# A graph layer's gathers: more columns fetched row by row on two queues, and edge features loaded for two groups at a time

## The chip, the cores and the metric

One core of a Trainium2 chip runs the whole kernel. A core has five engines with instruction streams of their own: TensorE (PE in the profile; its weight loads are shown as PEld), VectorE (DVE), ScalarE (ACT), GpSimd (POOL) and SyncE (SP, which does no arithmetic here and issues transfers). ScalarE, SyncE and GpSimd issue DMA transfers between HBM and the on-chip memory. The metric is the device time of the whole kernel in microseconds, the median of several runs.

## What is computed

A graph of 12,500 nodes with 64 features each and 200,000 edges, sorted by destination. Each edge makes a message from its two nodes' features and its own; messages are added up by destination, and the nodes are updated and normalised.

```python
def ssp(x): return jax.nn.softplus(x) - jnp.log(2.0)
nodes = node_state[edges].reshape(num_edges, -1)          # [x[src], x[dst]], 128 wide
gates = ssp(edge_state @ We1 + be1) @ We2 + be2
soft_cutoff = 1.0 - jax.nn.sigmoid(5.0 * (edges_distance - (CUTOFF - 1.5)))
h = ssp(nodes @ Wn1 + bn1) @ Wn2 + bn2
messages = h * gates * soft_cutoff
message_sum = jnp.zeros_like(node_state).at[edges[:, 1]].add(messages)
new_state = node_state + (ssp(message_sum @ Ws1 + bs1) @ Ws2 + bs2)
return layernorm(node_state + new_state)
```

## The kernel before

**Groups and columns.** The edges are cut into 391 groups of 512 (`NG`, `GE`). A group has two halves `h` of 256 edges and is laid out as `K = 4` columns of 128 edges. For a column, 128 rows of x are needed, one for each edge's source, 64 floats each. The main loop runs one step `i` for each group, with several groups in different stages in one step.

**Preparation** (the first 80 us or so) builds a table of x times the lower half of Wn1 in HBM (`table`), from which a window of 42 destination rows is loaded for each half of a group (`wns`, L235): since edges are sorted by destination, the destinations of a half lie within 42 nodes. During the preparation the gathers of the first 14 groups (`AHEAD`) are issued too.

**Fetching source rows.** Most columns are gathered by GpSimd: one indirect DMA for each column (`gather`, L202), reading 128 indices from `src_i`. In the main loop step `i` issues the gathers of group `i + 14`; the tile `xg` has 18 buffers. Some columns, listed by `slots_by_rows` (L101), are not gathered: column 3 of groups 36, 68, ... 388 is fetched by single rows on SyncE's queue and column 2 of the same groups on ScalarE's. `fetch(i, engine)` (L206) loads four row numbers into registers (L215) and issues four DMAs of one row (256 bytes) each (L219). SyncE's four stand behind the loads of the step; ScalarE's are split, two between the exp and the log of a step and two between the log and the copy behind it. A column takes 32 steps and is used from step g - 3 on; group 36's last rows are issued in step 31. ScalarE's rows are issued only in steps below 380 (`ends`).

**Loading.** `load(g)` (L225), called in step g - 5, issues on SyncE the edge features `eT` of one group (L228, 128 KB) and the two windows `wns` (L235), whose row numbers come from registers loaded for two groups at a time (L230). The loads wait until the scatter of group g - 11 is done.

**The order of a step**, written out by hand, for i < 380:

- SyncE: `load(i + 5)`, then four rows. GpSimd: the gathers of group i + 14.
- TensorE: `layer2_edge(i - 1)`, whose first matmul is L293; `layer1_edge(i + 1)` and `layer1_node(i + 1)` (L260, L262, L268); the scatter of group i - 3 (L320, a matmul with a one-hot matrix); `transposes(i + 3)` (L251); `layer2_node(i - 1)` (L303).
- L293 takes the waits of the step in one place (`needs`): the copy and the loads of group i + 1, and the gathers and one-hot of group i + 3.
- ScalarE: exp of group i + 1 (L279), two rows, log (L282), two rows, the copy of the transposed group i + 3 (`xcopy`, L256).
- VectorE: cutoff and message (L312, L316), the window's addition (L337), softplus (L287), the one-hot of group i + 5 (L241, and L244 for the columns fetched by rows).

Node blocks of 512 nodes (25 in all) are worked off between these, when the sums of their nodes are complete: a load and a store on SyncE's queue (L362, L416), some matmuls, and some work on ScalarE and VectorE. In the last ten steps (`CATCH_UP`) the lags shrink and the order changes, so that all stages end together; the last groups and the last node block follow the loop.

**Completion semaphores** of DMAs come from a pool: transfers issued by SyncE and ScalarE share some of them, and a new issue on a semaphore waits until the earlier transfer on it has landed.

Of the kernel before, what the change touches and what calls it, by code (L numbers as in the profile page):

```python
# [32 lines left out]

# [3 lines left out]

# [5 lines left out]
F32 = mybir.dt.float32  # L43
BF16 = mybir.dt.bfloat16
I32 = mybir.dt.int32
# [11 lines left out]
P = 128  # L57
D = 64
HE = 256
# [5 lines left out]
K = 4  # L65
# [7 lines left out]


BLOCK_STEPS = ((2, 3, 4, 4, 6, 7, 8, 9, 10, 14), (2, 3, 3, 4, 5, 6, 7, 8, 9, 10), (1, 2, 1, 2, 3))
ROWS = 4
CUTOFF = 5.0
EPS = 1e-5
LN2 = 0.6931471805599453
# [18 lines left out]
    return steps  # L98


def slots_by_rows(NG):  # L101

    return [(g, k) for k in (K - 1, K - 2) for g in range(P // ROWS + 4, NG - 2, P // ROWS)]


@with_exitstack
def gnn_resnorm_kernel(ctx: ExitStack, tc: tile.TileContext, a: dict, out: bass.AP, E: int):
    nc = tc.nc
    x = a["x"]
    N = x.shape[0]  # L110
    NG = a["eT"].shape[1]
# [8 lines left out]
    const = ctx.enter_context(tc.tile_pool(name="const", bufs=1))  # L120
    dram = ctx.enter_context(tc.tile_pool(name="dram", bufs=1, space=DRAM))
    loads = ctx.enter_context(tc.tile_pool(name="loads", bufs=LOADS + 2))
# [26 lines left out]
    packed, at = {}, 0  # L149
# [18 lines left out]
    xgs, xrs, eTs = {}, {}, {}  # L168
    made = {}

    def note(key, ins):
        made.setdefault(key, []).append(ins)
        return ins

    def behind(ins, *keys):

        for key in keys:
            for other in made.get(key, []):
                tc.add_manual_dep(ins.ins, other.ins.name,
                                  mybir.DependencyInfo(mybir.DependencyClass.Sync, mybir.DependencyReason.DATA),  # L180
                                  reason="one place of a step takes its waits")

    by_rows = slots_by_rows(NG)
    rows_i = const.tile([len(by_rows), P], I32, name="rows_i")
    half_of = {nc.sync: 0, nc.scalar: len(by_rows) // 2}

    def padding(g, k):
        return g * GE + k % 2 * HE + k // 2 * P >= E
# [14 lines left out]
                out=xg[:, k, :D], out_offset=None, in_=x,  # L203
                in_offset=bass.IndirectOffsetOnAxis(ap=src_i[:, g, k : k + 1], axis=0)))

    def fetch(i, engine, first=0, count=ROWS):  # L206

        n, r = divmod(i * ROWS + first, P)
        if i < 0 or n >= len(by_rows) // 2:
            return  # L210
        n += half_of[engine]
        if r == 0:
            xrs[by_rows[n]] = loads.tile([P, P], F32, name=f"xr{by_rows[n][1]}", bufs=2)
        if first == 0:
            _, row_at[engine] = nc.values_load_multi_w_load_instructions(  # L215
                rows_i[n : n + 1, r : r + ROWS], engines=[engine.engine], min_val=0, max_val=N - 1,
                skip_runtime_bounds_check_because="src holds rows of x")
        for j in range(count):
            note(("gather", by_rows[n][0]), engine.dma_start(xrs[by_rows[n]][r + j : r + j + 1, :D],  # L219
                                                             x[bass.ds(row_at[engine][first + j], 1), :]))  # L220

    row_at = {}
    bases = {}

    def load(g):  # L225
        eTs[g] = loads.tile([P, HE], F32, name="eT")
        old = ("scatter", g - LOADS - 2 - 4)
        behind(note(("load", g), nc.sync.dma_start(eTs[g], a["eT"][:, g, :])), old)  # L228
        if g % 2 == 0:
            _, at = nc.values_load_multi_w_load_instructions(  # L230
                base_i[0:1, 2 * g : 2 * g + 4], engines=[SP], min_val=0, max_val=N - 1,
                skip_runtime_bounds_check_because="they were clamped to these bounds")
            bases[g], bases[g + 1] = at[:2], at[2:]
        for h in range(2):
            behind(note(("load", g), nc.sync.dma_start(wns[D:DW, g % REST, h, :], table[bass.ds(bases[g][h], W), :])),  # L235
                   old)
# [17 lines left out]
    def xcopy(g):  # L254
        xT = work.tile([DW, K, P], F32, name="xT", bufs=3)
        note(("xcopy", g), nc.scalar.copy(xT, xTs[g]))  # L256
        xTs[g] = xT.rearrange("f (t h) e -> f h t e", h=2)
# [169 lines left out]
    with tc.manual_schedule():  # L427
# [4 lines left out]
        with tc.tile_pool(name="prep", bufs=1) as prep:  # L432
# [10 lines left out]

            for i in range(3):
                load_x(i)
            nc.sync.dma_start(rows_i, a["rows"])
            dist = cut.rearrange("p g k -> p (g k)")
            nc.sync.dma_start(dist, a["dist_l"])
            dst_i = rel.bitcast(I32)
# [50 lines left out]
            for i, w in enumerate((we2[:D, 0, :], wn2)):  # L500
                n = w.shape[0]
# [16 lines left out]
            rows = prep.tile([PIECES, 4, D], BF16, name="rows")  # L518
# [6 lines left out]
            for i in range(PARTS):  # L525
# [19 lines left out]
                if i == 2:  # L545
# [5 lines left out]
                    for t in range(2):  # L551
                        r = rel[:, :, 2 * t : 2 * t + 2]
# [3 lines left out]
        with tc.tile_pool(name="finish", bufs=1) as finish:  # L556
# [14 lines left out]
            parts, begun, complete, rest = {}, None, 0, []  # L571
# [9 lines left out]
            for i in range(-3, last - 1):  # L581
                now = parts.pop(i, [])
                early = [part for part in now if part.tensor]
                at(load, i + LOADS)
                fetch(i, nc.sync)
                if i >= 0:
                    at(gather, i + AHEAD, i < BEHIND)
                if i < ends:
                    needs = [("xcopy", i + 1), ("load", i + 1)]
                    needs += [(name, g) for g in ahead[i] for name in ("gather", "onehot")]  # L590
                    for g in second[i]:
                        layer2_edge(g, *needs)
                    if i >= -1:
                        zs[i + 1] = z_tile()
                        layer1_edge(i + 1)
                        for part in early:
                            part.tensor(tx_tile())
                    if i >= -1:
                        layer1_node(i + 1)
                    for n, g in enumerate(third[i]):  # L600
                        scatter(g, zs[i + 1][:, 1, HE + 2 * W * n : HE + 2 * W * (n + 1)])
                    at(exps, i + 1)
                    fetch(i, nc.scalar, 0, ROWS // 2)
                    at(logs, i + 1)
                    fetch(i, nc.scalar, ROWS // 2, ROWS // 2)
                    for g in ahead[i]:
                        transposes(g)
                        xcopy(g)
                    for g in second[i]:
                        layer2_node(g)  # L610
                    for g in second[i]:
                        hcut(g)
                        message(g)
                    for g in third[i]:
                        window(g)
                    for part in early:
                        part.others()
                    at(softplus, i + 1)
                else:
                    for g in ahead[i]:  # L620
                        transposes(g)
                        xcopy(g)
                    zs[i + 1] = z_tile()
                    layer1_edge(i + 1)
                    for part in early:
                        part.tensor(zs[i + 1][:, 1, HE:])
                    layer1_node(i + 1)
                    exps(i + 1)
                    logs(i + 1)
                    for g in second[i]:  # L630
                        layer2(g)
                        hcut(g)
                        message(g)
                    softplus(i + 1)
                    for g in third[i]:
                        scatter(g, tx_tile()[:, : 2 * W])
                        window(g)
                    for part in early:
                        part.others()
                for g in ahead[i]:  # L640
                    at(onehot, g + 2)
                for part in now:
                    if not part.tensor:
                        part.others()
                complete = third[i][-1] + 1 if third[i] else 0
                if blocks and complete >= blocks[0][1] - PREPARE and not begun:
                    begun = node_block(*blocks[0][0], finish)
                    begun.pop(0).others()
                if blocks and complete >= blocks[0][1]:
                    steps = next(steps for steps in BLOCK_STEPS if i + steps[-1] < last - 1)  # L650
                    for n, part in zip(steps, begun):
                        parts.setdefault(i + n, []).append(part)
                    rest = begun[len(steps) :]
                    blocks.pop(0)
                    begun = None
# [44 lines left out]
    with tc.If(far > 0), tc.tile_pool(name="outside", bufs=1) as o:  # L700
# [7 lines left out]
        with tc.For_i(0, NG, 1) as g:  # L708
# [14 lines left out]
            for k in range(K):  # L723
                for i in range(2):
                    nc.gpsimd.indirect_dma_start(
                        out=xg[:, k, i, :], out_offset=None, in_=x,
# [20 lines left out]
            v = gh.rearrange("p (i k d) -> p i k d", i=2, k=K)  # L747
# [12 lines left out]
            for b in range(NBL):  # L760
# [5 lines left out]
                part = sums[:D, b * NB : (b + 1) * NB]  # L766
# [8 lines left out]
def layouts(inputs):  # L775
# [8 lines left out]
    NG = -(-E // GE)  # L784
# [3 lines left out]
    def padded(v, n, fill):  # L788
        return np.concatenate([v, np.full((n - v.shape[0],) + v.shape[1:], fill, v.dtype)])
# [4 lines left out]

    out = {"x": np.ascontiguousarray(x)}
    out["src_l"] = lanes(src, 0)
    out["rows"] = np.ascontiguousarray(out["src_l"].reshape(P, NG, K)[(slice(None), *zip(*slots_by_rows(NG)))].T)
    out["dst_l"] = lanes(dst, dst[-1])
    out["dist_l"] = lanes(dist, 1e6)
    out["dst_h"] = np.ascontiguousarray(padded(dst, NR * P * HE, dst[-1]).reshape(NR, P, HE).transpose(1, 0, 2))  # L800
# [42 lines left out]
```

## Time and profile before

| what | value |
|---|---|
| median of 3 runs | 1989.88 us |
| lowest and highest run | 1989.77, 1997.46 us |
| profiled execution | 1994.42 us |
| its span | 1992.6 us |
| mean granted TensorE clock in it | 0.977 |

| transfers | issued by | count |
|---|---|---|
| gathers of one column, `xg` | POOL | 1539 |
| single rows, `xr` | SyncE | 1536 |
| single rows, `xr` | ScalarE | 1520 |
| edge features, `eT`, 128 KB | SyncE | 391 |
| windows, `wns`, 21 KB | SyncE | 782 |

Some groups of the page, as line, busy time, mean of one, idle time before it:

| line | work | busy us | mean ns | idle us before |
|---|---|---|---|---|
| L279 | ScalarE, exp | 317.4 | 810 | 659.1 |
| L282 | ScalarE, log | 365.9 | 933 | 304.4 |
| L256 | ScalarE, copy | 222.4 | 569 | 24.4 |
| L293 | TensorE, first matmul of a step | 148.9 | 381 | 103.1 |
| L287 | VectorE, softplus | 372.8 | 951 | 24.3 |

How to read the profile: times are microseconds from the span's start. In a view in order of time a line gives the start, the duration, the engine, the source line, the operation, out<-in, and how many were merged; in brackets the idle time of the engine before it and what the profile takes to have ended it. "SPq" and "ACTq" are the queues of SyncE and ScalarE, where issuing a transfer takes time but does not count as busy. A group's line gives the count, then busy time and mean ns of one, then idle time before and what ended it. In the views of one line of code the three numbers after a count are the shortest, median and longest duration in ns. What ended a wait is inferred from semaphores and can name a bystander.

### The profile page before, as it was taken

The numbers are of one execution on the slowest core, as the hardware profiler recorded it, in microseconds if no ns is written. First come the engines' busy times: TensorE is split into PE (matmuls) and PEld (weight loads), VectorE is DVE, ScalarE is ACT, GpSimd is POOL, SyncE is SP. The second block draws the span as 40 slices with busy tenths as digits, with TensorE's granted clock in tenths as the row PEclk, the third lists the DMA queues.
The fourth block names the chain that finished last, engine by engine and source line by source line (L and its number), as shares of the span: only waits on it lengthen the run. The fifth ranks groups of instructions, "written<-read, shape, count | busy, mean of one in ns | idle before, by whom it ended". The sixth has DMA issues, their size and how long they took to land.

```text
span 1992.6 us, 46151 instructions
## 1 busy us (share of the span) xinstructions
PE 1843.2 (92%) x11373; PEld 1531.6 (77%) x11373; DVE 1082.5 (54%) x2756; ACT 925.0 (46%) x1318; POOL 1463.8 (73%) x1543
## 2 busy tenths in 40 slices
PE   5899999999998998989999899999999999999996
PEld 4788788888777777777777777777887787787775
DVE  4455455555554554645555555555565555555554
ACT  1355455554444444544444444454454444455442
POOL 6777777777777777777777777777777777777770
PEclk9999899999999999999999999999899999999996
DMA  8422222222222222222232222232232222222230
GB/s 239 131 67 70 63 68 70 69 66 69 67 66 65 65 67 63 66 66 63 68 72 62 68 67 68 63 73 63 68 73 68 68 69 68 69 68 68 71 74 10
DMA packets 173687, 143.41 MB, mean 72 GB/s; under 512 B 49324, under 2 KB 145776, under 8 KB 173415
## 3 DMA queue, kind: packets, MB, share of 16 engines
q1 hardware_dynamic: 119758, 87.95, 15.3%
q0 software_dynamic: 49248, 50.53, 13.2%
q10 hardware_dynamic: 4408, 1.90, 0.4%
q8 instruction: 97, 1.59, 0.3%
q14 instruction: 176, 1.43, 0.2%
HBM read 130.57 MB, written 9.63 MB: 70 GB/s over the span
## 4 chain that ended last, share of the span: by engine, by line
PE 73%; SPq 8%; DMA 7%; issue 5%; DVE 2%; ACT 2%; ACTq 1%; POOL 1%; DVEq 0%; POOLq 0%
PE z L268 15%; PE gh L303 11%; PE gh L297 11%; PE z L262 10%; PE z L320 7%; PE tx L251 6%; PE gh L293 6%; DMA xr<-in_x 6%; PE z L260 3%; SPq L235 3%; SPq L219 2%; SPq L215 2%; PE z L530 2%; ACT u L279 2%; DVE h L312 1%
## 5 line engine op out<-in xcount | busy, mean ns | idle before, releaser
L202 POOL DMA_INDIRECT xg<-in_x,src_i x1539 | 1463.6, 951 | 477.8 <-issue 336.7
L279 ACT ACTIVATE u<-z 128x768 f32<-128x768 f32 x392 | 317.4, 810 | 659.1 <-PE z L320 625.3
L312 DVE TENSOR_TENSOR h<-gh,cut 128x256 f32<-128x256 f32 x391 | 166.1, 425 | 686.1 <-PE gh L303 669.8
L282 ACT ACTIVATE u<-u,one 128x768 f32<-128x768 f32 x392 | 365.9, 933 | 304.4 <-DMA xr<-in_x 294.6
L268 PE MATMUL z<-xT,wns 106*128 106x256 f32 x1564 | 415.9, 389 | 0.0
L303 PE MATMUL gh<-consts,s 128*128 128x64 f32 x3128 | 397.8, 271 | 0.0
L303 PEld LDWEIGHTS gh<-consts,s 128*128 128x128 f32 x3128 | 386.5, 194 | 0.0
L287 DVE SCALAR_TENSOR_TENSOR s<-u,z 128x768 f32<-128x768 f32 x392 | 372.8, 951 | 24.3 <-ACT u L282 7.2
L268 PEld LDWEIGHTS z<-xT,wns 106*128 106x128 f32 x1564 | 302.1, 195 | 44.8 <-ACT xT L256 0.7
L297 PE MATMUL gh<-consts,s 128*128 128x128 f32 x1564 | 280.8, 302 | 0.0
L262 PE MATMUL z<-eT,consts 128*128 128x256 f32 x782 | 277.7, 437 | 0.0
L297 PEld LDWEIGHTS gh<-consts,s 128*128 128x128 f32 x1564 | 205.8, 191 | 92.0 <-issue 91.4
L320 PEld LDWEIGHTS z<-xg,msg 128*128 128x128 f32 x1512 | 234.7, 196 | 21.6
L293 PE MATMUL gh<-row,ones 3*128 3x512 bf16 x391 | 148.9, 381 | 103.1 <-DMA xr<-in_x 47.8
L251 PE MATMUL tx<-consts,xg 128*106 128x128 f32 x1540 | 238.0, 278 | 4.0 <-DVE xg L241 2.7
L256 ACT COPY xT<-tx 106x512 f32<-106x512 f32 x391 | 222.4, 569 | 24.4 <-PE tx L251 15.3
L320 PE MATMUL z<-xg,msg 128*128 128x84 f32 x1512 | 221.6, 269 | 0.0
L337 DVE TENSOR_TENSOR sums<-sums,z 64x42 f32 x756 | 148.5, 196 | 129.9 <-issue 116.7
L251 PEld LDWEIGHTS tx<-consts,xg 128*106 128x106 f32 x1540 | 182.9, 144 | 5.2 <-DVE xg L241 3.0
L316 DVE TENSOR_TENSOR msg<-gh,h 128x256 f32<-128x256 f32 x391 | 165.9, 424 | 13.4
L262 PEld LDWEIGHTS z<-eT,consts 128*128 128x128 f32 x782 | 117.7, 190 | 47.6 <-issue 1.5
L293 PEld LDWEIGHTS <-ones 3*128 3x128 bf16 x391 | 35.5, 91 | 140.2 <-issue 122.1
(101 smaller groups left out, 685.5 us busy)
## 6 DMA issues: line engine op xcount, KB each, us to landing
eT<-in_eT SPq DMA_DIRECT2D x391, 128.0 KB
xg<-in_x,src_i POOLq DMA_INDIRECT x1539
xr<-in_x SPq DMA_DIRECT2D x1536, 0.2 KB
xr<-in_x ACTq DMA_DIRECT2D x1520, 0.2 KB
wns<-table SPq DMA_DIRECT2D x782, 21.0 KB
table<-tb SPq DMA_DIRECT2D x14, 448.0 KB
sums<-in_xT SPq DMA_DIRECT2D x7, 455.0 KB
y<-in_x SPq DMA_DIRECT2D x24, 128.0 KB
```

The lines of the kernel that those rows point to most:

```text
L202: note(("gather", g), nc.gpsimd.indirect_dma_start(out=xg[:, k, :D], out_offset=None, in_=x, in_offset=bass.IndirectOffsetOnAxis(ap=src_i[ ...
L251: nc.tensor.transpose(tx[:, k, :], row, ident)
L256: note(("xcopy", g), nc.scalar.copy(xT, xTs[g]))
L262: nc.tensor.matmul(zs[g][:, 0, :HE], we1.rearrange("a h d -> a (h d)"), eTs[g], start=False, stop=True, skip_group_check=True)
L268: nc.tensor.matmul(zn, wns[:, g % REST, h, :], xTs[g][:, h], start=True, stop=True, skip_group_check=True)
L279: nc.scalar.activation(us[g][:, part], z_of(g)[:, part], AF.Exp)
L282: nc.scalar.activation(us[g][:, part], us[g][:, part], AF.Ln, bias=one)
L287: nc.vector.scalar_tensor_tensor(ss[g].rearrange("p i t e -> p (i t e)")[:, part], us[g][:, part], BIG, z_of(g)[:, part], OP.min, OP.max)
L293: first = nc.tensor.matmul(gh, ones3[:, :P], row3.rearrange("q i k d -> q (i k d)"), start=True, stop=False, skip_group_check=True)
L297: nc.tensor.matmul(v[:, 0, t], ss[g][:, 0, t, :], we2, start=False, stop=False, skip_group_check=True)
L303: nc.tensor.matmul(ghs[g][:, 1, 2 * t + h, :], ss[g][:, 1 + h, t, :], wn2, start=False, stop=h == 1 and t == 1, skip_group_check=True)
L320: ins = nc.tensor.matmul(sc, msgs[g][:, 2 * t : 2 * t + 2, :].rearrange("p h f -> p (h f)"), xgs[g][:, 2 * t : 2 * t + 2, D:DW], start=t = ...
```

## The change

- `SYNC_ROWS = 5` and `SCALAR_ROWS = 6` take the place of `ROWS = 4`: rows a step by SyncE (column 3) and by ScalarE (column 2).
- The two lists are now separate and at different groups. A column's group is the step in which its rows are complete plus 6 (before, plus 4): column 3 of groups 32, 58, 83, ... 365 (14 columns) by SyncE, column 2 of groups 28, 49, 70, ... 369 (17 columns) by ScalarE. The row numbers lie in two small arrays, loaded in the preparation by two transfers instead of one.
- ScalarE's six rows are issued in three pairs: behind exp, behind log, and (new) behind the copies of the step.
- `load(g)` loads `eT` for two groups in one transfer of 256 KB in every even step; four such buffers take the place of seven of half the size. The windows are loaded as before.

```diff
-ROWS = 4
+SYNC_ROWS = 5
+SCALAR_ROWS = 6
...
-def slots_by_rows(NG):
-    return [(g, k) for k in (K - 1, K - 2) for g in range(P // ROWS + 4, NG - 2, P // ROWS)]
+def slots_by_rows(NG, k, rows):
+    ready = [-(-(n + 1) * P // rows) + 6 for n in range(NG)]
+    return [(g, k) for g in ready if g < NG - 2]
...
-    rows_i = const.tile([len(by_rows), P], I32, name="rows_i")
-    half_of = {nc.sync: 0, nc.scalar: len(by_rows) // 2}
+    lists, by_rows = {}, []
+    for engine, name, k, rows in ((nc.sync, "rows_sync", K - 1, SYNC_ROWS), (nc.scalar, "rows_scalar", K - 2, SCALAR_ROWS)):
+        lists[engine] = rows, slots_by_rows(NG, k, rows), const.tile(a[name].shape, I32, name=name)
+        by_rows += lists[engine][1]
...
-    def fetch(i, engine, first=0, count=ROWS):
+    def fetch(i, engine, part=0, parts=1):
+        rows, slots, rows_i = lists[engine]
+        at = i * rows
+        total = min(rows, len(slots) * P - at)
+        if i < 0 or total <= 0:
             return
+        if part == 0:
+            n, first = divmod(at, rows_i.shape[1])
             _, row_at[engine] = nc.values_load_multi_w_load_instructions(
-                rows_i[n : n + 1, r : r + ROWS], engines=[engine.engine], min_val=0, max_val=N - 1,
+                rows_i[n : n + 1, first : first + total], engines=[engine.engine], min_val=0, max_val=N - 1,
                 skip_runtime_bounds_check_because="src holds rows of x")
+        for j in range(part * rows // parts, min(total, (part + 1) * rows // parts)):
+            n, r = divmod(at + j, P)
+            if r == 0:
+                xrs[slots[n]] = loads.tile([P, P], F32, name=f"xr{slots[n][1]}", bufs=2)
+            note(("gather", slots[n][0]), engine.dma_start(xrs[slots[n]][r : r + 1, :D],
+                                                           x[bass.ds(row_at[engine][j], 1), :]))
...
     def load(g):
-        eTs[g] = loads.tile([P, HE], F32, name="eT")
         old = ("scatter", g - LOADS - 2 - 4)
-        behind(note(("load", g), nc.sync.dma_start(eTs[g], a["eT"][:, g, :])), old)
+        if g % 2 == 0:
+            n = min(2, NG - g)
+            both = loads.tile([P, 2, HE], F32, name="eT", bufs=4)
+            behind(note(("load", g), nc.sync.dma_start(both[:, :n], a["eT"][:, g : g + n, :])), old)
+            for j in range(n):
+                eTs[g + j] = both[:, j]
...
-            nc.sync.dma_start(rows_i, a["rows"])
+            nc.sync.dma_start(lists[nc.sync][2], a["rows_sync"])
+            nc.sync.dma_start(lists[nc.scalar][2], a["rows_scalar"])
...
-                    fetch(i, nc.scalar, 0, ROWS // 2)
+                    fetch(i, nc.scalar, 0, 3)
                     at(logs, i + 1)
-                    fetch(i, nc.scalar, ROWS // 2, ROWS // 2)
+                    fetch(i, nc.scalar, 1, 3)
                     for g in ahead[i]:
                         transposes(g)
                         xcopy(g)
+                    fetch(i, nc.scalar, 2, 3)
```

More of the change, by code (lines that the diff above doesn't have):

```diff
@@ L35 @@
 from contextlib import ExitStack
-from math import ceil, sqrt
+from math import ceil, lcm, sqrt
 import concourse.bass as bass
@@ L181, in behind @@
                                   reason="one place of a step takes its waits")
-    by_rows = slots_by_rows(NG)
-    rows_i = const.tile([len(by_rows), P], I32, name="rows_i")
-    half_of = {nc.sync: 0, nc.scalar: len(by_rows) // 2}
+    lists, by_rows = {}, []
+    for engine, name, k, rows in ((nc.sync, "rows_sync", K - 1, SYNC_ROWS), (nc.scalar, "rows_scalar", K - 2, SCALAR_ROWS)):
+        lists[engine] = rows, slots_by_rows(NG, k, rows), const.tile(a[name].shape, I32, name=name)
+        by_rows += lists[engine][1]
     def padding(g, k):
@@ L204, in gather @@
                 in_offset=bass.IndirectOffsetOnAxis(ap=src_i[:, g, k : k + 1], axis=0)))
-    def fetch(i, engine, first=0, count=ROWS):
-        n, r = divmod(i * ROWS + first, P)
-        if i < 0 or n >= len(by_rows) // 2:
+    def fetch(i, engine, part=0, parts=1):
[3 more added lines that the diff above has]
+        if i < 0 or total <= 0:
             return
[L211 to L214, printed above, removed]
+        if part == 0:
+            n, first = divmod(at, rows_i.shape[1])
             _, row_at[engine] = nc.values_load_multi_w_load_instructions(
-                rows_i[n : n + 1, r : r + ROWS], engines=[engine.engine], min_val=0, max_val=N - 1,
+                rows_i[n : n + 1, first : first + total], engines=[engine.engine], min_val=0, max_val=N - 1,
                 skip_runtime_bounds_check_because="src holds rows of x")
-        for j in range(count):
-            note(("gather", by_rows[n][0]), engine.dma_start(xrs[by_rows[n]][r + j : r + j + 1, :D],
-                                                             x[bass.ds(row_at[engine][first + j], 1), :]))
+        for j in range(part * rows // parts, min(total, (part + 1) * rows // parts)):
[4 more added lines that the diff above has]
+                                                           x[bass.ds(row_at[engine][j], 1), :]))
     row_at = {}
@@ L796, in layouts @@
     out["src_l"] = lanes(src, 0)
-    out["rows"] = np.ascontiguousarray(out["src_l"].reshape(P, NG, K)[(slice(None), *zip(*slots_by_rows(NG)))].T)
+    for name, k, rows in (("rows_sync", K - 1, SYNC_ROWS), ("rows_scalar", K - 2, SCALAR_ROWS)):
+        v = out["src_l"].reshape(P, NG, K)[(slice(None), *zip(*slots_by_rows(NG, k, rows)))].T.reshape(-1)
+        n = lcm(P, rows)
+        out[name] = padded(v, -(-v.shape[0] // n) * n, 0).reshape(-1, n)
     out["dst_l"] = lanes(dst, dst[-1])
```

## The prediction

> **What bounds the kernel now.** I read four views: the page's summary, the instructions of POOL in order of time, TensorE's first matmul of each step (L293, which waits for everything a step needs), and SyncE's queue. The page first:
>
> ```profile
> PE 1843.2 (92%) x11373; PEld 1531.6 (77%) x11373; DVE 1082.5 (54%) x2756; ACT 925.0 (46%) x1318; POOL 1463.8 (73%) x1543
> PE 73%; SPq 8%; DMA 7%; issue 5%; DVE 2%; ACT 2%; ACTq 1%; POOL 1%; DVEq 0%; POOLq 0%
> L202 POOL DMA_INDIRECT xg<-in_x,src_i x1539 | 1463.6, 951 | 477.8 <-issue 336.7
> ```
>
> By the busy shares and the chain of waits, TensorE is the bound and POOL has a quarter of its time free. That reading fails at the third line: busy 1463.6 and idle 477.8 make 1941.4 us, nearly the whole span. The time-ordered view of POOL shows what the idle time is:
>
> ```profile
> 1000.18 0.94 POOL L202 DMA_INDIRECT xg<-in_x,src_i  x1 [0.30 <-issue]
> 1001.43 0.94 POOL L202 DMA_INDIRECT xg<-in_x,src_i  x1 [0.30 <-issue]
> 1002.68 0.94 POOL L202 DMA_INDIRECT xg<-in_x,src_i  x1 [0.30 <-issue]
> ```
>
> Every gather is followed by the same 0.30 us, whatever is named as its end. The page of waits has only 9.4 us of longer stops on POOL (2.8 for src_i, 6.6 for L195), all in the preparation. So one gather costs (1941.4 - 9.4) / 1539 = 1.255 us and POOL never rests: four are 5.02 us a step, less the 24 columns fetched by rows, 4.94 us a step. TensorE on its own is quicker. Its L293 in the early steps, and later:
>
> ```profile
> 182.29 0.39 PE L293 MATMUL gh<-row,ones 3*128 3x512 bf16 x1
> 186.64 0.39 PE L293 MATMUL gh<-row,ones 3*128 3x512 bf16 x1
> ```
>
> ```profile
> 904.00 0.37 PE L293 MATMUL gh<-row,ones 3*128 3x512 bf16 x1 [0.75 <-DMA xr<-in_x]
> 908.78 0.37 PE L293 MATMUL gh<-row,ones 3*128 3x512 bf16 x1 [0.38 <-PE gh L303]
> ```
>
> Early there is no idle time and a step takes 4.35 us, because the gathers made during the preparation are a stock of some ten groups. TensorE eats it up by group 92 (about 490 us). From then on L293 stops again and again. The names given ("DMA xr", "PE gh") are not believable: landings of POOL's gathers are hardly told by this profile, and the gather of the fourth column needed at 908.78 ended on POOL at 907.02 (counted off in order from the first), 1.76 us earlier; for 904.00 it is 902.02, 1.98 us. Wherever L293 waits, I find this same distance. It is the landing of the gather. From group 92 to the end of the wait, POOL sets the time.
>
> Where does that end? In the last ten steps TensorE's work is reordered, and there the order of time shows
>
> ```profile
> 1907.23 0.37 PE L293 MATMUL gh<-row,ones 3*128 3x512 bf16 x1 [0.22 <-PE gh L303]
> ...
> 1915.26 0.39 PE L293 MATMUL gh<-row,ones 3*128 3x512 bf16 x1
> ```
>
> ```profile
> 1904.25 1.03 POOL L202 DMA_INDIRECT xg<-in_x,src_i  x1 [0.30 <-issue]
> ```
>
> The stop at 1907.23 stands 1.95 us behind the end (1905.28) of the last gather of group 382: the same landing. At 1915.26 the last gather of group 383 is 5 us old, and later ones are older when they are used (the last of all ends at 1941.87, and its transposes come at 1963.5). So what counts is how many gathers stand before the end of group 382; from 1907 on a fixed tail of TensorE and VectorE, 87 us, follows.
>
> **The change, part by part.** *Gathers.* SyncE's list: a column is full every 128/5 = 25.6 steps, at groups 32, 58, ... 365: 14. ScalarE's: every 21.3 steps, at 28, 49, ... 369: 17. Together 31 in place of 24, so 1532 gathers. Of the old 24, two are in group 388, behind the point that counts; of the new 31 none is. Up to group 382 there are 31 - 22 = 9 fewer: 9 x 1.255 = **11.3 us**. Over the whole list it would be 7 x 1.255 = 8.8 us; POOL's last gather then ends about 1933, and its group is used about 1952, so nothing waits there.
>
> *Rows.* SyncE issues 1792 instead of 1536, ScalarE 2176 instead of 1520. None is on the path as long as both queues keep pace. SyncE's queue, early, when it ran behind and was held by nothing else:
>
> ```profile
> 171.04 0.36 SPq L228 DMA_DIRECT2D eT<-in_eT  x1
> 171.59 0.82 SPq L235 DMA_DIRECT2D wns<-table  x2
> 173.22 1.50 SPq L219 DMA_DIRECT2D xr<-in_x  x4
> ...
> 188.40 0.37 SPq L228 DMA_DIRECT2D eT<-in_eT  x1
> ```
>
> From 171.04 to 188.40 are four steps: 4.34 us each, with waits of 0.19 in it (5.1 us in the 26 steps from 100 to 215 us). Four rows run from the first issue to the end of the fourth in 1.50, so one is (1.50 - 0.23)/3 = 0.42. The change adds one row (+0.42) and removes every second eT issue (0.36 and some 0.1 around it, halved: -0.23): 4.34 + 0.42 - 0.23 = 4.53, and 0.06 for the node blocks' loads and stores, 4.59 us. The step of the gathers becomes 5.02 - 1.255 x (1/25.6 + 1/21.33) = 4.91. SyncE keeps 0.3 us of room.
>
> *The register loads* before the rows take five and six values instead of four. The loads show no price per value:
>
> ```profile
> L215 SPq TENSOR_LOAD <-rows_i x384: 469/562/740, 85.3 to 1927.8; - x192
> L215 ACTq TENSOR_LOAD <-rows_i x380: 484/490/531, 82.7 to 1910.4; - x190
> ```
>
> ```profile
> L698 SPq TENSOR_LOAD <-far_i x1: 478/478/478, 1987.5 to 1987.5; - x1
> ```
>
> One value took 0.478 us and four took 0.49 to 0.56. I take nothing; the other end is a second load of 0.56. The Trainium skill speaks against the change here: "Runtime: NRT & Kernel Launch", section "Instruction fetch mechanics", puts such a load at about 200 ns for each register, from HBM. By it, as an estimate, SyncE's step would be 4.79 and ScalarE's longer by 0.4, still under the gathers' step; these four-value loads from SBUF at 0.49 us do not follow it.
>
> *Waits inside the queues.* The row DMAs of both queues and SyncE's loads share a few completion semaphores, and an issue waits for the landing of an earlier DMA. Between 500 and 1900 us SyncE stops 186 us in 283 steps for these, 0.66 a step. I read most of it as slack: early, with TensorE at 4.35, the waits were only 0.19. With 13.5 DMAs a step instead of 11 the bounds are 0.19 x 13.5/11 = 0.23 and 0.66 x 13.5/11 = 0.81 a step; SyncE's step is 4.63 or 5.21. I take the lower, since in the row nearest to a queue at its limit it was 0.19.
>
> *ScalarE.* Two more issues stand behind xcopy, whose 0.57 us cover part of them: a pair takes 0.61 us from its first issue to the end of its second (the row's time in the ordered view at 903.76) and 0.14 of register work ahead, 0.75 in all, so 0.2 us remain. They come out of the idle time before the next exp, 625.3 us in 369 steps, 1.7 us each, so nothing on the path. Without that cover exp, log and softplus come 0.75 us later, and they are needed one step on.
>
> *The rest.* eT in 256 KB every second step carries the same bytes; the odd group arrives a step earlier, the even one at most by the time of another 128 KB later, under four steps (about 19 us) between issue and use. Seven more VectorE copies of 0.19 us lie in its idle time. A column's last row now comes four steps ahead of L293's need instead of two; the one long stop on it (3.15 us at 224.65, near step 33) goes, but falls in the stretch where the stock of gathers covers it. One more small load in the preparation delays dist and dst by one issue of about 0.4 us, far from POOL's start.
>
> **Sum.** The profiled execution took 1994.42 us (span 1992.6 and 1.8 around it): 1994.42 - 11.3 = 1983.1. The median of the runs, 1989.88, is 4.5 lower; the same step from there gives **1978.6 us**.
>
> **Rivals.** *(A) The forecast*, 1978.6. *(B) SyncE's queue takes POOL's place.* Place: the rows at L219, locked to ScalarE's rows by the shared semaphores. Lateness is first absorbed: about 15 us by the four steps between a column's last row and its use (19.6, less the 4.1 by which SyncE's rows of a step end behind its L293: 908.10 against 904.00), and about 10 us by the 24 steps from the last row to group 382, where a step of gathers is 5.02 and one of TensorE 4.6 (4.94 less L293's idle 103.1 us over 300 steps). Rows run for 358 steps, so it decides from 4.91 + 25/358 = 4.98 us a step. At the upper waits (5.21) it costs 0.23 x 358 = 82 us; halfway, 5.10, 43 us: 2022. For it: SyncE has only 0.3 us of room, and waits of up to 4.2 us occur. Against it: 4.34 us held without slack early. *(C) Only seven count*, because TensorE falls behind near group 382 or the tail starts to wait for the last gather: 1989.88 - 8.8 = 1981.1. Against it, the 16 to 22 us that the last two groups' gathers are old when they are used. *(D) TensorE is the bound as its 92% say*, and nothing comes of it: 1989.9. Against it, 4.35 us steps wherever gathers are in stock and stops at L293 in the rest.
>
> **How the numbers follow.** A 0.57, B 0.20, C 0.13, D 0.10. The likeliest gives 1978.6. The executions shown spread from 1989.77 to 1997.46, and in the last 33 us the clock is at half, so some us of A can go either way: its own range is 1973 to 1984. To leave out no more than 2 in 10 the range reaches into B up to 5.04 us a step: 1973 to 1999. Half a per cent (about what a measurement here can tell from no change) is 9.9 us, or 1979.9: A lies just beyond it, and I give it 0.7 of A and some of C: faster 0.45; same (the rest of A, most of C, D, the edge of B) 0.34; slower 0.21.
>
> **What would show it.** Right: 1532 gathers at 1.25 us without longer gaps; L293's stops still about 1.8 to 2 us behind a gather; group 382's last gather near 1894; rows 1792 and 2176; TENSOR_LOAD near 0.5 us. Wrong: SyncE's rows near 5 us a step without idle, long stops of L293 with POOL far ahead, or POOL with gaps over 0.3 us.

## The result, and the profile after

The changed kernel takes 2427.32 us (median of 4 runs, 2419.54 to 2435.27) against 1990.41 us for the kernel before (median of 4 runs, the three listed above among them): a ratio of 1.2186, with a 95% interval of 1.2136 to 1.2235. It is 437 us slower, where 1978.6 was forecast and the range ended at 1999. The profiled execution took 2429.64 us. (Five runs made while the kernel before itself took 2571 or 2597 us are not used; they stand at the end of the experiments.)

The page of the changed kernel:

```profile
PE 2099.0 (86%) x11373; PEld 1723.6 (71%) x11373; DVE 1068.8 (44%) x2763; ACT 941.2 (39%) x1318; POOL 1453.4 (60%) x1536
PE 46%; SPq 21%; DMA 10%; issue 10%; ACTq 7%; ACT 5%; DVE 1%; DVEq 0%
L205 POOL DMA_INDIRECT xg<-in_x,src_i x1532 | 1453.2, 949 | 883.3 <-PE z L330 398.5
```

POOL made its 1532 gathers in the same 0.95 us each, but its idle time grew from 477.8 to 883.3 us, and most of the new part ends with TensorE's scatter (L330, the old L320): GpSimd now waits for its buffers, the gathers are no longer the bound. In the chain SyncE's queue went from 8% to 21%, ScalarE's queue from 1% to 7%. TensorE does the same 11,373 matmuls in 256 us more busy time; its granted clock fell from 0.977 to 0.870.

The view of the waits names two new ones (line, what it waited for, us in total, times, longest):

```profile
ACT u L292 <- DMA xr<-in_x: 771.1, 360, 5.5
```

```profile
SPq L236 <- PE z L330: 287.3, 132, 6.5
```

In the kernel before, what the same two instructions waited for most (the log at L282, the load of eT at L228):

```profile
ACT u L282 <- DMA xr<-in_x: 294.6, 368, 1.1
```

```profile
SPq L228 <- DMA xr<-in_x: 91.8, 124, 3.9
```

ScalarE's log now waits behind a row that ScalarE itself issues, for up to 5.5 us; before, it was 294.6 us in all and at most 1.1. SyncE's load of eT now waits for TensorE's scatter, which it hardly ever did (0.4 us in all between 500 and 1900 us). The chain of waits through one step, in order of time (start, us, what), ties them together:

```profile
1004.26 0.80 PE z L330 x4
1005.07 0.37 SPq L236
...
1007.06 1.34 SPq L218
...
1008.59 1.57 DMA xr<-in_x
1010.18 0.45 ACTq L225
...
1011.06 0.05 ACT u L292
...
1012.14 0.59 ACT xT L266
...
1013.33 0.58 PE gh L303
```

The scatter of step 150 ends; SyncE, at that moment in its step 153, may load eT, reads its registers (1.34 us), and issues a row; that row lands 1.57 us later; only then does ScalarE issue its first row of step 150, at 1010.18, and only then comes the log (1011.06), behind which stand the copy and TensorE's next L303. Nothing in the data makes ScalarE's row wait for SyncE's. They carry the same completion semaphore, and ScalarE's issue waits for it. For each of ScalarE's rows one can look up in the trace which DMA used its semaphore last. Done for steps 60 to 340 of both traces (the node blocks' transfers left out), this shows how the order is new:

```
ScalarE's rows                              before    after
behind a SyncE DMA of a later step           0%        61%   (of three steps later, nearly all)
behind a SyncE DMA of the same step         22%         0%
median time from SyncE's first row of a
step to ScalarE's first row of it          0.4 us    18.5 us
```

SyncE's queue runs three steps ahead of TensorE, as far as the load's wait for an old scatter lets it, and the order in which the semaphores were given out when the program was built has it there as well. So ScalarE's step waits for a landing of SyncE's step three later, which waits for TensorE's scatter of the present step: a loop, with 5.1 us from the scatter's end to ScalarE's row in the step shown. Along the whole chain of the changed kernel the path runs from TensorE through SyncE's queue to ScalarE 131 times, in the median with 5.5 us on the way; in the chain of the kernel before it never does. The second thing that the chain shows is the register load:

```profile
L218 ACTq TENSOR_LOAD <-rows_scalar x363: 506/1150/1755, 81.8 to 2268.0; - x182
L218 SPq TENSOR_LOAD <-rows_sync x359: 697/1327/1497, 83.9 to 2225.8; - x180
```

The medians are 1.15 and 1.33 us instead of 0.49 and 0.56. Sorted by the address of the first value, SyncE's five values take 0.78 us when it is a multiple of 16 bytes (one step in four) and 1.33 otherwise; ScalarE's six take 0.94 (one in two) and 1.53. Four values a step always began at such a multiple (four numbers are 16 bytes).

The line also gives SyncE's pace: first and last start, 359 loads, so (2225.8 - 83.9)/358 = 5.98 us a step. The same for the kernel before: (1927.8 - 85.3)/383 = 4.81.

### The profile page after: what moved, and what is told of

The parts are those of the page before. It is cut to its first block, busy times and chain, and to the rows that moved or that the text cites. A ratio compares the mean times of both kernels' runs of the same rounds, so it can differ in the third digit from the quotient of the medians.

```text
span 2427.7 us, 48622 instructions
## 1 busy us (share of the span) xinstructions
PE 2099.0 (86%) x11373; PEld 1723.6 (71%) x11373; DVE 1068.8 (44%) x2763; ACT 941.2 (39%) x1318; POOL 1453.4 (60%) x1536
## 4 chain that ended last, share of the span: by engine, by line
PE 46%; SPq 21%; DMA 10%; issue 10%; ACTq 7%; ACT 5%; DVE 1%; DVEq 0%
PE z L278 11%; SPq L218 7%; PE z L272 7%; PE gh L307 7%; DMA xr<-in_x 6%; ACTq L225 5%; SPq L245 5%; PE z L330 5%; PE gh L313 5%; SPq L225 4%; PE gh L303 3%; ACT xT L266 3%; PE tx L261 3%; DMA wns<-table 3%; SPq L240 3%
## 5 line engine op out<-in xcount | busy, mean ns | idle before, releaser
L205 POOL DMA_INDIRECT xg<-in_x,src_i x1532 | 1453.2, 949 | 883.3 <-PE z L330 398.5
L278 PE MATMUL z<-xT,wns 106*128 106x256 f32 x1564 | 494.2, 447 | 0.0
L313 PE MATMUL gh<-consts,s 128*128 128x64 f32 x3128 | 423.9, 282 | 0.0
L313 PEld LDWEIGHTS gh<-consts,s 128*128 128x128 f32 x3128 | 419.0, 208 | 0.0
L278 PEld LDWEIGHTS z<-xT,wns 106*128 106x128 f32 x1564 | 351.2, 226 | 64.0 <-ACT xT L266 0.7
L303 PE MATMUL gh<-row,ones 3*128 3x512 bf16 x391 | 157.5, 403 | 258.2 <-ACT xT L266 232.7
L272 PE MATMUL z<-eT,consts 128*128 128x256 f32 x782 | 314.7, 488 | 0.0
L307 PE MATMUL gh<-consts,s 128*128 128x128 f32 x1564 | 307.3, 324 | 0.0
L330 PEld LDWEIGHTS z<-xg,msg 128*128 128x128 f32 x1512 | 277.8, 229 | 33.3
L307 PEld LDWEIGHTS gh<-consts,s 128*128 128x128 f32 x1564 | 226.0, 208 | 99.5 <-issue 98.9
L261 PE MATMUL tx<-consts,xg 128*106 128x128 f32 x1533 | 272.9, 306 | 27.3 <-ACT xT L266 23.2
L330 PE MATMUL z<-xg,msg 128*128 128x84 f32 x1512 | 256.3, 300 | 0.0
L303 PEld LDWEIGHTS <-ones 3*128 3x128 bf16 x391 | 35.7, 91 | 298.2 <-ACT xT L266 258.9
L261 PEld LDWEIGHTS tx<-consts,xg 128*106 128x106 f32 x1533 | 210.6, 161 | 31.9 <-ACT xT L266 26.7
```

The source lines that it names most:

```text
L205: note(("gather", g), nc.gpsimd.indirect_dma_start(out=xg[:, k, :D], out_offset=None, in_=x, in_offset=bass.IndirectOffsetOnAxis(ap=src_i[ ...
L261: nc.tensor.transpose(tx[:, k, :], row, ident)
L272: nc.tensor.matmul(zs[g][:, 0, :HE], we1.rearrange("a h d -> a (h d)"), eTs[g], start=False, stop=True, skip_group_check=True)
L278: nc.tensor.matmul(zn, wns[:, g % REST, h, :], xTs[g][:, h], start=True, stop=True, skip_group_check=True)
L303: first = nc.tensor.matmul(gh, ones3[:, :P], row3.rearrange("q i k d -> q (i k d)"), start=True, stop=False, skip_group_check=True)
L307: nc.tensor.matmul(v[:, 0, t], ss[g][:, 0, t, :], we2, start=False, stop=False, skip_group_check=True)
```

## The experiments

Two theories: LOCK, the loop through the shared semaphores; LOADS, the dearer register loads, which bind SyncE's queue whatever the order. Times in one table; "before" is the kernel before, run beside each. The changed kernel's time is the median of 4 runs and e13's of 12; the others are single runs.

```
run                what differs                         us       before    SyncE's step, us
changed kernel                                          2427.3   1990.4    5.98
e8_aligned         loads aligned                        2298.4   1991.8    5.63
e9_hold            SyncE's rows held                    2115.6   1991.8    5.16
e10_hold_aligned   both                                 1989.6   1991.8    4.80
e11_rows44         rows 4 and 4                         1990.5   1991.8    4.78
e7_shift           kernel before, loads misaligned      2010.3   1996.4    4.88
e12_rows46         rows 4 and 6                         2225.8   1993.6    5.40
e13_hold46         rows 4 and 6, held, aligned          1988.1   1993.6    4.78
```

SyncE's step is worked out from each run's line of register loads as above.

**The cost of the loads alone.** The kernel before, with its four values off the boundary:

```diff
-    rows_i = const.tile([len(by_rows), P], I32, name="rows_i")
+    rows_i = const.tile([len(by_rows), P + 4], I32, name="rows_i")
...
-                rows_i[n : n + 1, r : r + ROWS], ...
+                rows_i[n : n + 1, r + 1 : r + 1 + ROWS], ...
...
-            nc.sync.dma_start(rows_i, a["rows"])
+            nc.sync.dma_start(rows_i[:, 1 : P + 1], a["rows"])
```

> The kernel before the change, with the row numbers moved by four bytes in their array, so that every register load before the rows begins off a 16-byte boundary; rows, order and semaphores as before. The cost of a load alone: by the changed kernel's 1.33 us for five and 1.53 for six, four values should take about 1.1 instead of 0.49 to 0.56. SyncE's step becomes 4.40 + 0.6 = 5.0 us, at or just over the gathers' 4.94, with no cushion of six steps: LOCK: 1990 to 2040 us. LOADS: the load is the main cost of the change, 2150 or more. If the kernel before, run beside it, is far from 1990, only the load's duration is read.

The loads' view of this run:

```profile
L215 SPq TENSOR_LOAD <-rows_i x384: 1037/1136/1326, 84.1 to 1953.3; - x192
L215 ACTq TENSOR_LOAD <-rows_i x380: 1092/1115/1427, 80.3 to 1930.2; - x190
```

Twice the duration for the same four values, by four bytes of address. The time rose by 14 us, 0.7%, in this one run. By themselves the loads are not 437 us.

**Loads made cheap in the changed kernel, order kept.**

```diff
+STRIDE = 8
...
-            n, first = divmod(at, rows_i.shape[1])
+            n, first = divmod(i * STRIDE, rows_i.shape[1])
...
-        n = lcm(P, rows)
-        out[name] = padded(v, -(-v.shape[0] // n) * n, 0).reshape(-1, n)
+        v = padded(v, -(-v.shape[0] // rows) * rows, 0).reshape(-1, rows)
+        v = np.concatenate([v, np.zeros((v.shape[0], STRIDE - rows), v.dtype)], axis=1).reshape(-1)
+        out[name] = padded(v, -(-v.shape[0] // 512) * 512, 0).reshape(-1, 512)
```

> The changed kernel with the row numbers of a step stored 8 apart, so that each register load begins at a multiple of 32 bytes (five values still 5, six still 6); the planned order of the semaphores is the same as in the changed kernel. LOCK (ScalarE's row issues stand, on the shared semaphores, behind SyncE's rows of three steps later, which stand behind TensorE's scatter of the present step): the loop stays and gets shorter by at most 0.41 + 0.30 us a step: 2160 to 2350 us. LOADS (the dearer register loads alone make SyncE's queue the bound): 1980 to 2010.

```profile
L219 ACTq TENSOR_LOAD <-rows_scalar x363: 510/944/1112, 82.0 to 2142.7; - x182
L219 SPq TENSOR_LOAD <-rows_sync x359: 674/779/970, 84.9 to 2099.8; - x180
```

The medians fell to 0.94 and 0.78 as expected, and 129 us with them; 2298 us remain. LOCK holds, LOADS alone does not: the share of ScalarE's rows behind a later step of SyncE is still 61%.

**The order changed, loads kept dear.**

```diff
-            note(("gather", slots[n][0]), engine.dma_start(...))
+            row = note(("gather", slots[n][0]), engine.dma_start(...))
+            if engine is nc.sync and j == 0:
+                behind(row, ("xcopy", i + 2))
```

> The changed kernel with SyncE's first row of step i waiting for ScalarE's copy of group i+2 (the copy of the step before). A wait is added and nothing taken away, but SyncE's rows are now planned beside ScalarE's rows of the same step, not three steps ahead. LOCK: the loop through the scatter is gone, and SyncE's queue at about 5.25 us a step with its dear loads is left: 2020 to 2120. LOADS: 2400 or more, as nothing gets cheaper.

One more wait, and the kernel is 312 us quicker. In its trace 66% of ScalarE's rows stand behind a SyncE DMA of the same step and 9% behind a later one; SyncE's first row comes 1.3 us ahead of ScalarE's, not 18.5. What is left is SyncE's queue at 5.16 us a step, near the 5.25 of the expectation; the waits that the profile shows on it between 300 and 1800 us come to only 23 us.

**Both.**

> Both: the hold and the aligned register loads (0.78 and 0.94 us). LOCK: with the loop gone and SyncE's queue at 4.84 us, POOL's gathers bound the time again: 1978 to 2000. A loop of another kind that the hold itself makes (SyncE's rows behind ScalarE's copy, ScalarE's rows behind SyncE's) would show as 2050 or more.

```profile
L206 POOL DMA_INDIRECT xg<-in_x,src_i x1532 | 1456.4, 951 | 477.0 <-issue 367.7
L295 ACT ACTIVATE u<-u,one 128x768 f32<-128x768 f32 x392 | 366.0, 934 | 595.1 <-DMA xr<-in_x 591.8
```

1989.6 us: POOL's idle time is back at 477.0, its constant 0.30 us a gather. The two mends are nearly additive: the hold is worth 312 us with dear loads and 309 with cheap ones (2298.4 to 1989.6), the loads 129 and 126. Together they account for the whole loss. But what nine gathers fewer bring doesn't show: this one run can't be told from the kernel before. The last gather of group 382 (counted off in order) ended at 1894.9 us, as forecast, 10.4 us earlier than before; but TensorE's first matmul that needs it (L306, the old L293) came 4.9 us behind it and not 1.95, and about 20 us behind its gathers in mid-run. The log still waits 591.8 us for rows. The queues now set a step of 4.80 us, only just shorter than POOL's 4.91: TensorE falls behind early, while gathers are in stock, and makes it up only slowly, to the last.

**Rows back to four each**, everything else of the change kept (pairs of groups for eT, six steps ahead):

```diff
-SYNC_ROWS = 5
-SCALAR_ROWS = 6
+SYNC_ROWS = 4
+SCALAR_ROWS = 4
```

> The changed kernel with four rows a step on each queue (lists still six steps ahead, pairs of groups for the features kept); 22 columns up to group 382 as before the change. ScalarE's rows are planned behind rows of the same step or the one before; loads of four values at 16-byte boundaries near 0.5 us. LOCK and LOADS both: 1982 to 2000 us. If the 256 KB transfer of two groups were the cause: over 2100.

1990.5 us. The 256 KB transfers and the longer lead cost nothing that shows here. So the loss comes with the number of rows.

**Rows four and six**: SyncE's queue light, ScalarE's as in the change.

```diff
-SYNC_ROWS = 5
+SYNC_ROWS = 4
```

> The changed kernel with SyncE's rows back at four a step (its loads then begin at 16-byte boundaries and take about 0.55 us) and ScalarE's kept at six. As built, ScalarE's rows still stand on their semaphores behind SyncE's rows of three steps later. LOCK: SyncE's queue needs only about 4.15 us a step, under the gathers' 4.94, and the kernel is slow all the same: 2200 to 2400. LOADS: SyncE's queue has its room back, 1980 to 2010.

SyncE's loads and its waits in this run:

```profile
L218 SPq TENSOR_LOAD <-rows_sync x352: 462/561/788, 84.0 to 1979.4; - x176
```

```profile
SPq L236 <- PE z L330: 447.4, 182, 7.2
```

SyncE's load is cheap again (0.56 us) and it stands idle for 447 us in front of eT alone, and the kernel takes 2225.8 us: a queue with time to spare, in a loop. 46% of ScalarE's rows are behind a later step of SyncE.

**A version with both mends and fewer rows**: four and six, loads aligned, the hold.

> Four rows by SyncE and six by ScalarE, register loads aligned, SyncE's first row held behind ScalarE's copy of the step before. 28 columns up to group 382 instead of 22. If the hold removes the loop and POOL's gathers are the bound: 6 x 1.255 = 7.5 us under the kernel before, 1980 to 1986 at a before of 1990. If the two queues still stand in each other's way at about 4.8 us a step, as in the run with both mends: 1986 to 1995.

1988.13 us (median of 12 runs, 1983.73 to 2000.71) against 1993.63 (17 runs): ratio 0.998, interval 0.9959 to 1.0. That counts as the same: it is quicker by anything between nothing and 8 us, so neither the full 7.5 us of six gathers nor none of it is excluded. The time lies in the second range of the expectation, but its trace does not look like that case. POOL is back to back:

```profile
L206 POOL DMA_INDIRECT xg<-in_x,src_i x1535 | 1461.7, 952 | 476.8 <-issue 337.9
```

From step 100 to about 345 L306 mostly stands 2 us behind the last gather that it needs, as L293 did before the change; near the end it is about 6 us. So POOL sets the time here through most of the run.

**Five runs that are not used.** Made while the kernel before, beside them, took 2571.2 us, and 2596.9 us for the second run with aligned loads.

The changed kernel with aligned loads, as e8_aligned, made twice: 2758.2 and 2785.0 us.

> The changed kernel with the row numbers of a step stored 8 apart, so that each register load begins at a multiple of 32 bytes (five values still 5, six still 6). In the changed kernel SyncE's load takes 0.78 us at a 16-byte boundary and 1.33 elsewhere, ScalarE's 0.94 and 1.53. Theory LOCK (ScalarE's row issues stand, on the shared semaphores, behind SyncE's rows of three steps later, which stand behind TensorE's scatter of the present step): the loop stays and only gets shorter by at most 0.41 + 0.30 us a step, so 2160 to 2350 us. Rival LOADS (the dearer register loads alone make SyncE's queue the bound at 5.25 us a step): the queue falls to 4.84, and the time to 1980 to 2010. In both, loads near 0.78 and 0.94.

> The same kernel as e1_aligned, once more: in that session the kernel before took 2571 us instead of 1990, and SyncE's queue shows hundreds of stops of 0.71 us between its register instructions that the first two profiles do not have, so its times can't be set beside those. Expected if the kernel before is near 1990: LOCK 2160 to 2350 us, LOADS 1980 to 2010.

Edge features loaded for single groups, the rows as in the change: 2866.4 us.

```diff
-        if g % 2 == 0:
-            n = min(2, NG - g)
-            both = loads.tile([P, 2, HE], F32, name="eT", bufs=4)
...
+        eTs[g] = loads.tile([P, HE], F32, name="eT")
+        behind(note(("load", g), nc.sync.dma_start(eTs[g], a["eT"][:, g, :])), old)
```

> The changed kernel with the edge features loaded for one group at a time again (128 KB, seven buffers), rows 5 and 6 kept. LOCK: nothing of the loop goes, SyncE has 0.23 us a step more: 2400 to 2520. Rival PAIR (the 256 KB transfer is what comes late or blocks the queue): back to 1980 to 2010.

Rows back to four each, as e11_rows44: 2536.8 us.

> The changed kernel with four rows a step on each queue (lists still six steps ahead, pairs of groups for the features kept). Columns at groups 38, 70, ... 358 on both, 22 up to group 382 as before the change. LOCK and LOADS: planned order of the semaphores as before the change (ScalarE's rows behind rows of the same step or the one before), loads of four values at 16-byte boundaries near 0.5 us: 1982 to 1998 us. PAIR: over 2100.

SyncE's rows held, as e9_hold: 2785.8 us.

> The changed kernel with SyncE's first row of step i waiting for ScalarE's copy of group i+2 (the copy of the step before). One wait is added and nothing taken away; but SyncE's rows are then planned beside ScalarE's rows of the same step, not three steps ahead. LOCK: the loop through the scatter is gone, and what is left is SyncE's queue at about 5.25 us a step with its dear loads: 2020 to 2120. LOADS: 2400 or more, as nothing gets cheaper.

Nothing follows from them for the theories: in all five profiles SyncE's own queue has hundreds of stops of about 0.7 us, where the other profiles have a few dozen at most, and no theory speaks of these. The kernel with single loads was not run again, so what single loads do beside five and six rows was not measured. But e10 keeps the pairs beside five and six rows and the loss is gone, as e11 keeps them beside four and four: the pairs alone do not make it.

## Why the prediction was wrong

*The bound of the kernel before* was read rightly: POOL's gathers, behind busy shares that point to TensorE. Its unbroken gathers return in e10, e11 and e13 at 1988 to 1991 us. For POOL itself the sum came out in e10: group 382's last gather at 1894.9, where near 1894 was forecast. That the kernel gains 11.3 us by it was never shown: in e10 the queues took POOL's place, and e13, with six gathers fewer, can't tell 7.5 us from none.

*The step that failed* is "Waits inside the queues", with the words "I take the lower". I scaled SyncE's waits by the number of DMAs, as if the order in which two queues hand semaphores to each other were fixed. It was not: with more rows on ScalarE the built program has SyncE three steps ahead, and each wait on a shared semaphore became a wait for another engine's future work. I had the order of the kernel before in its trace (every predecessor from the same step or the one before) and did not ask what would keep it so. My upper bound, 0.81 us a step, was of the wrong kind: the waits that count were ScalarE's, 771 us in front of the log. About 310 of the 437 us went when the order was mended.

*The second step that failed* is "The register loads", priced at nothing with 0.56 us as the other end. SyncE's grew by 0.77 us in the median and ScalarE's by 0.66. I compared one value with four and read off "no price per value"; the four stood on a 16-byte boundary, and I did not see that five and six values, packed one step behind the other, cannot always do so. This is worth 126 to 129 us here. "Runtime: NRT & Kernel Launch" of the Trainium skill, section "Instruction fetch mechanics", gives about 200 ns a register, and I set it aside. The runs go with it for each further value, beyond four aligned ones (0.56, 0.78 and 0.94 us for four, five and six) and off the boundary (1.13, 1.33 and 1.53): 0.16 to 0.22 us. They go against it for four aligned values (0.49 to 0.56 us instead of 0.8). It should have stood in the range.

*Rival B* named the right place, rows locked to rows by shared semaphores, and the wrong size and direction: it had SyncE as the engine out of time, deciding from 4.98 us a step with 25 us of cushion. e12 is slow with SyncE idle; and the cushion was not there, since a late row holds ScalarE's log at once, long before the column is needed. With the hold, 5.16 us a step gave 2115.6 (B's sum, 1978.6 + 0.18 x 358, gives 2043) and 4.80 gave 1989.6. These two runs put the point near POOL's own pace.

*ScalarE* was said to pay 0.2 us out of idle time. The log's idle time in front of it rose from 304 to 781 us instead; what I had not counted is that an issue waiting for a semaphore stands in the same stream as the log.

*TensorE's clock* adds to the loop, and I had no term for it. In the chain of the changed kernel the four matmuls of L278 just ahead of that scatter take 1.4 us or more in 100 of 203 steps (1.71 in the step shown) and 0.86 to 0.87 in nearly all the others; the same four in the chain of the kernel before (its L268) take that long in 13 of 311. In those steps the scatter that releases SyncE comes later. The hold, which touches no matmul, brought the granted clock from 0.870 back to 0.963, so the low clock went with the loop; how it comes about, and how much of the 310 us it is, was not separated.

*Rivals C and D* and the last steps could not be tested: in the changed kernel and in e10 POOL was not the bound, and in e13, where it was, the interval of 0 to 8 us can't tell them from A.

What makes the order of the built program tip, so that SyncE stands three steps ahead, was not settled: e11 (4 and 4 rows) does not tip, e12 (4 and 6) does, so SyncE's fifth row is not needed for it.

## What to carry to other kernels

When two engines' queues draw their DMAs' completion semaphores from one pool, ask of every added transfer behind whose transfer it will wait, and what that one waits for; more transfers can change the order of the whole program, and one extra wait that keeps the queues in step was worth about 310 us here. Read a small price per item only from rows with the same alignment as the new ones. And a queue's spare time is no cover when an engine's own work stands behind the issue in the same stream.

## What was not expected of the hardware

- A register load's duration depends on the address: four values took 0.49 to 0.56 us at a multiple of 16 bytes and 1.12 to 1.14 us four bytes further; five took 0.78 us at such a multiple and 1.33 at 4, 8 or 12 bytes beyond; six took 0.94 and 1.53. Four aligned values cost hardly more than the single one of L698 (0.48 us).
- TensorE's granted clock was lower wherever the loop stood: 0.870 in the changed kernel, 0.898 with cheap loads, 0.923 with rows 4 and 6, against 0.977 before and 0.958 to 0.982 in the runs without the loop.
